# A first norm for two batches only, the other six and three pieces of preparation woven into the attention

## The chip, the cores and the metric

The kernel runs on one NeuronCore of a Trainium2 chip. The metric is device time in microseconds (us) of one execution, as a median over executions. A core has five instruction streams that run side by side and wait for one another by semaphores: TensorE (PE, matrix products and transposes through the array), VectorE (DVE), ScalarE (ACT, functions from tables, copies, scalings), GpSimd (POOL) and SyncE (SP, which issues most DMA transfers). PEld is PE's loading of weights, which overlaps its matmuls. Each stream is worked off in its own order.

## The reference, cut to what matters

Four layers act on x of 8 batches with 512 tokens of 128 values. Each layer does

```python
xn = _layernorm(x, axis=-1)      # (x - mean) / sqrt(var + 1e-5)
s = attention(xn)
g = _silu(ffn(xn))
x = x + s * g
```

The change concerns the first layer and preparation for later ones. The attention of layer 0 has 16 heads of 8 values and a sliding window of 64 tokens: a block of 64 queries sees its own and the previous block of keys, masked, with a softmax over 128 keys, and a projection out. The feed-forward part of layer 0 multiplies by six 128x128 weights, which come as integers and are decoded as `q / 7.5 - 1`, times a scale per group of 16, plus a low-rank product. The attention of layer 1 mixes each token with the one before by three vectors of weights. The attention of layer 3 needs per head a few scalars (softplus, sigmoid, reciprocals of six parameters).

## The kernel before, in words

x lies transposed in SBUF, 128 values on the partitions and 4096 tokens along the free axis, as do xn (normed) and s (attention out). Eight loads of 256 KB fill x. A tile of the norm is one batch, 512 tokens, so there are eight tiles.

**The first norm**, `layer_norm`: for each tile PE multiplies four blocks of 128 tokens by a centring matrix `cmat`, which gives rows of tokens less their mean in PSUM (`ps_c`); ACT squares them (`sq`), DVE sums (`var`) and adds epsilon, POOL takes the power -0.5 (`rstd`), DVE multiplies (`row`), PE transposes back (`ps_t`) and ACT copies into `xn`. The tiles follow one another with the later parts two and three tiles behind. PE, DVE, ACT and POOL run it in program order (`in_order`).

**Beside it**: `l0_decode` turns the integers of the six weights into `wt` by three DVE operations of 128x768. `l1.fill` has ACT issue the loads of the expert weights (`m1_w13`, `m1_w2`), then compute `td`, `rest`, the six mixing weights `wm` and a halved weight. `l3_scalars` stands in the source after the feed-forward part, but its operations are not held in order, and the scheduler puts them early: in the profile they run before the first scores (lines 2740 to 2777). The loads of weights for layers 2 and 1 (`L2Consts`, `L1Consts`) stand on SP's queue ahead of the layer-0 weights `a0_w`.

**The attention**, `l0_attention`: every engine works in program order, which is written out by hand. A batch has eight units u; a unit is 128 queries by 8 heads. In unit u, in this order: `turned(u)` transposes the eight exponentiated score blocks on PE (`tp`), four to a bank, and ACT copies them out (`pt`); in every second unit DVE divides the finished sums (`rec`, `o`); `scores(u + 3)` has PE multiply (`sc`), DVE scale and mask (`e`) and take the maximum (`mx`), POOL subtract it; `out_rows` transposes `o` (`tpo`, `ot`); ACT takes the exponential of unit u + 2; `weigh(u)` multiplies with the values on PE (`av`); in unit 1 of a batch `finish` projects the batch before (`ps_o`, `s`). Last, `next(todo)` does one step of the projections of the next batch: in unit 0 the keys (`ps_k`, then four pieces `kb` in turn by DVE and ACT, the first two here and the other two in unit 1), in unit 2 the queries (`ps_q`, `q`), in units 3 and 4 the values (`ps_v`, `vw`). The generator `l0_low_rank` adds the low-rank products to `wt` in unit 6 of the later batches. All of tp, tpo, ps_k, ps_q, ps_v and ps_o take their banks from one pool of three PSUM banks (`p_t`); scores have two buffers of two banks, the sums one bank.

Numbers of units below are of the whole attention (u = 0 to 63), "unit 0 to 7" within a batch is u modulo 8. Nearly all lines carry L83 in the profile, since the helper that keeps program order issues them; groups are told apart by the names of tiles.

Of the kernel before, what the change touches and what calls it, by code (L numbers as in the profile page):

```python
# [9 lines left out]
F32 = mybir.dt.float32  # L10
# [17 lines left out]
class Net:  # L28
# [110 lines left out]
        self.nc.gpsimd.tensor_tensor(r, var, self.neg_half.to_broadcast([P, n]), ALU.pow)  # L139
        return r  # L140

    def layer_norm(self, x, xn, gamma=None, beta=None, banks=(5, 3), free=False):

        nc, tc = self.nc, self.tc
        K = TB // P
        pe, dve, act, pool = (
            e if free else self.in_order(e)
            for e in (nc.tensor, nc.vector, nc.scalar, nc.gpsimd)
        )
        with tc.tile_pool(name="ln_s", bufs=3) as sp, tc.tile_pool(  # L150
            name="ln_p", bufs=banks[0], space=PSUM
        ) as pp, tc.tile_pool(name="ln_t", bufs=banks[1], space=PSUM) as tp:
# [38 lines left out]

            for t in range(NTB + 3):
                if t < NTB:
                    centre(t)
                    spread(t)
                if 2 <= t < NTB + 2:
                    scale(t - 2)
                if t >= 3:
                    turn(t - 3)
                    keep(t - 3)  # L200
# [46 lines left out]
            )  # L247


def l0_attention(net, xn, s_out, p0, w, bias):  # L250


    nc, tc = net.nc, net.tc
# [3 lines left out]
    with ExitStack() as st:  # L257
# [146 lines left out]
            scores(u)  # L404
        act.activation(e[0], e[0], AF.Exp)
        act.activation(e[1], e[1], AF.Exp)
        todo = iter(())
        for u in range(N + 2):
            if u < N and u % U == 0 and u // U + 1 < B:
# [14 lines left out]
            if u >= U and u % U == 1:  # L424
                finish(u // U - 1)
            next(todo, None)
            if u == 4 * U:
                low = net.prep.l0_low_rank(
                    p0, lambda name: p_t.tile([P, S], F32, tag="t", name=name), pe, dve, act
                )  # L430
            if u > 4 * U and u % U == 6:
                next(low, None)


L0_FFN = (
# [288 lines left out]
class L1Consts:  # L724
    E = 8

    def __init__(self, net, st):
        nc, tc, E = net.nc, net.tc, self.E
        self.net = net
        self.p1 = p1 = st.enter_context(tc.tile_pool(name="a1_c", bufs=1))  # L730
        self.rw = net.load(p1, "m1_r")
        self.eb = p1.tile([P, E], F32, tag="eb", name="eb")
        nc.sync.dma_start(self.eb, net.ins["m1_eb"].partition_broadcast(P))
# [3 lines left out]

    def fill(self):
        net, nc, p1, E = self.net, self.net.nc, self.p1, self.E
        act = net.in_order(nc.scalar)  # L740
        self.w13 = net.load(p1, "m1_w13", act)
        self.w2 = net.load(p1, "m1_w2", act)

        w, par = self.w, self.par
        self.td = td = p1.tile([P, 1], F32, tag="td", name="td")
        act.activation(td, par[:, 0:1], AF.Exp)
        act.activation(td, td, AF.Copy, scale=-1.0)
        self.tf = par[:, 1:2]
        self.wm = wm = p1.tile([P, 3, 2, P], F32, tag="wm", name="wm")
        self.rest = rest = p1.tile([P, 3], F32, tag="rest", name="rest")  # L750
        act.activation(rest, par[:, 2:5], AF.Identity, scale=-1.0, bias=net.ones[:, 0:1])
        for i in range(3):
            act.activation(wm[:, i, 0, :], w[:, i, :], AF.Copy, scale=par[:, 2 + i : 3 + i])
            act.activation(wm[:, i, 1, :], w[:, i, :], AF.Copy, scale=rest[:, i : i + 1])
        act.activation(w[:, 3, :], w[:, 3, :], AF.Copy, scale=0.5)

        def counting(tag, shape, pattern, base=0, channel=0):
            i = p1.tile(shape, I32, tag=tag + "_i", name=tag + "_i")
# [17 lines left out]
        self.keep = p1.tile([P, E, NTILE], F32, tag="keep", name="keep")  # L776
        nc.gpsimd.memset(self.keep, 1.0)
        nc.gpsimd.memset(self.keep[:, :, 0:1], 0.0)


def l1_layer(net, x, xn, s_out, consts, l2):
# [552 lines left out]
class L2Consts:  # L1334
# [4 lines left out]
    def __init__(self, net, st):  # L1339
# [2 lines left out]
            self.W, self.H, self.HD, self.LH, self.LD, self.NL, self.CH  # L1342
        )
        self.net = net
        self.p1 = p1 = st.enter_context(tc.tile_pool(name="a2_c", bufs=1))
        self.w = net.load(p1, "a2_w")
        self.wqt = net.load(p1, "a2_qt")
        self.wg = net.load(p1, "a2_g")
# [1312 lines left out]
class Prepared:  # L2661
# [26 lines left out]
            )  # L2688
        self.f0_wt = p1.tile([P, 6, P], F32, tag="wt", name="wt")

    def l0_decode(self):
        nc, wt, qw, sc = self.net.nc, self.f0_wt, self.qw, self.sc
        nc.vector.tensor_copy(wt, qw)
        nc.vector.tensor_scalar(wt, wt, 1.0 / 7.5, -1.0, ALU.mult, ALU.add)
        nc.vector.tensor_tensor(wt, wt, sc, ALU.mult)

    def l0_low_rank(self, p1, bank, pe, dve, act):

# [28 lines left out]
            dve.tensor_scalar(w0, w0, mean, None, ALU.subtract)  # L2727
            yield

    def l3_scalars(self):  # L2730

        net, nc, p1 = self.net, self.net.nc, self.p1
        H, DH = 16, 64
# [3 lines left out]
        )  # L2737
        sp = p1.tile([P, 4, H], F32, tag="sp", name="sp")
        raw = par[:, 1:5, :]
        nc.vector.scalar_tensor_tensor(sp, raw, -1.0, raw, ALU.mult, ALU.min)  # L2740
        nc.scalar.activation(sp, sp, AF.Exp)
        nc.scalar.activation(sp, sp, AF.Ln, bias=net.ones[:, 0:1])
        nc.vector.scalar_tensor_tensor(sp, raw, 0.0, sp, ALU.max, ALU.add)
        sig2, eta2, gam2, nu = (sp[:, i, :] for i in range(4))

        def vec(tag):
            return p1.tile([P, H], F32, tag=tag, name=tag)

        mu, nmu, v_e2, v_0, coef = vec("mu"), vec("nmu"), vec("v_e2"), vec("v_0"), vec("coef")
        nc.scalar.activation(mu, par[:, 0, :], AF.Exp, scale=-1.0)  # L2750
        nc.vector.tensor_scalar(mu, mu, 1.0, None, ALU.add)
        nc.vector.reciprocal(mu, mu)
        nc.vector.tensor_scalar(mu, mu, 1e-4, None, ALU.add)
        nc.vector.tensor_scalar(nmu, mu, -1.0, None, ALU.mult)

        nc.vector.tensor_scalar(v_e2, nmu, 2.0, None, ALU.mult)
        nc.vector.reciprocal(v_e2, v_e2)
        nc.vector.tensor_tensor(v_e2, v_e2, sig2, ALU.mult)
        nc.vector.tensor_tensor(v_0, eta2, gam2, ALU.add)
        nc.vector.tensor_tensor(v_0, v_0, v_e2, ALU.subtract)  # L2760
        nc.vector.tensor_scalar(coef, nu, float(DH), -0.5, ALU.add, ALU.mult)
        nc.vector.tensor_tensor(coef, coef, par[:, 5, :], ALU.mult)


        norm_0 = vec("norm_0")
        nc.vector.tensor_tensor(norm_0[0:64], nu[0:64], v_e2[0:64], ALU.mult)
        nc.vector.tensor_tensor(norm_0[64:128], nu[64:128], v_0[64:128], ALU.mult)
        cs, ncs, inv_cs, g_v = vec("cs"), vec("ncs"), vec("inv_cs"), vec("g_v")


        nc.vector.scalar_tensor_tensor(cs, coef, -1.0, coef, ALU.mult, ALU.max)
        nc.vector.tensor_scalar(cs, cs, 1e-18, 2e-18, ALU.is_lt, ALU.mult)
        nc.vector.tensor_tensor(cs, cs, coef, ALU.add)
        nc.vector.tensor_scalar(ncs, cs, -1.0, None, ALU.mult)
        nc.vector.reciprocal(inv_cs, cs)
        nc.vector.tensor_scalar(g_v, coef, -1.0, -0.5 * DH, ALU.mult, ALU.add)
        nc.vector.tensor_tensor(g_v, g_v, inv_cs, ALU.mult)
        self.scalars = nu, nmu, v_e2, v_0, norm_0, ncs, inv_cs, g_v


def network(tc, ins, out):
    with ExitStack() as ctx:
# [12 lines left out]
        with tc.tile_pool(name="prep_0", bufs=1) as p0:  # L2795
            w0, b0 = net.load(p0, "a0_w"), net.load(p0, "a0_b")
            prep.l0_load(p0)
            net.layer_norm(x, xn)
            prep.l0_decode()
            l2.fill()  # L2800
            l1.fill()
            l0_attention(net, xn, s, p0, w0, b0)
            l0_ffn(net, x, xn, s, l1)
        prep.l3_scalars()
        l1_layer(net, x, xn, s, l1, l2)
        st1.close()
        l2_layer(net, x, xn, l2)
# [82 lines left out]
```

## Time and profile before

| What | us |
|---|---|
| median of 12 runs (lowest, highest) | 2343.67 (2334.29, 2349.53) |
| the profiled execution, its own time | 2333.47 |
| its span | 2331.7 |
| busy PE / DVE / ACT / POOL in the span | 2172.8 / 1995.2 / 1857.1 / 1577.5 |
| first norm's first product | 4.08 |
| first scores of the attention | 42.00 |
| last projection out of the attention (s) | 315.40 |

Lines of the profile give start and length in us, the engine, the line of the kernel, the operation, the tiles written and read with shapes, and in brackets how long the engine sat idle before and what released it. "PEclk" is the clock that was granted to PE, as a share of full speed. A matmul in float32 shows as two PE instructions, a transpose as one. The profile is one execution; its own time differs from the median of the runs.

### The profile page before, as it was taken

To read this page: it belongs to the slowest core of one execution; us is meant where nothing else is said; L and a number is where in the kernel's file an instruction comes from. 1 tells how busy PE (TensorE), PEld (TensorE's weight loads), DVE (VectorE), ACT (ScalarE), POOL (GpSimd) and SP (SyncE) were. 2 spreads that over 40 slices of the span, in tenths; PEclk is the share of its full clock that TensorE was granted. 3 is DMA by queue.
4 is the path that set the end of the run, shared out by engine and by line. 5 is a ranking of instruction groups with operands and counts; after the bars stand their busy time and mean duration, and the time that the engine had idled before them with its cause. 6 is when DMAs were issued, how large, how long until landed. Compare 5 with 4: busy or idle time off the path is not lost.

```text
span 2331.7 us, 48954 instructions
## 1 busy us (share of the span) xinstructions
PE 2172.8 (93%) x17762; PEld 1518.3 (65%) x17762; DVE 1995.2 (86%) x3579; ACT 1857.1 (80%) x3906; POOL 1577.5 (68%) x1414
## 2 busy tenths in 40 slices
PE   5999998999987999769999999999999999999888
PEld 4666676556534666537777767777777777777676
DVE  4677778875787999679999999999999999999655
ACT  4666665555544899849999999999999999999875
POOL 4444435355276788666788887888887888887555
PEclk7999988999998999999999999999999999999999
DMA  4000001012210000144444344344443444433100
GB/s 144 2 2 2 2 1 37 9 54 71 44 49 13 7 17 16 57 115 107 109 107 109 94 105 110 101 106 107 105 105 102 99 111 112 104 95 87 40 1 37
DMA packets 91617, 156.94 MB, mean 67 GB/s; under 512 B 20144, under 2 KB 44464, under 8 KB 91120
## 3 DMA queue, kind: packets, MB, share of 16 engines
q1 hardware_dynamic: 86736, 140.95, 23.1%
q0 software_dynamic: 4352, 8.92, 1.6%
q10 hardware_dynamic: 288, 3.93, 0.4%
q8 instruction: 142, 2.33, 0.4%
q14 instruction: 99, 0.81, 0.1%
HBM read 30.52 MB, written 12.06 MB: 18 GB/s over the span
## 4 chain that ended last, share of the span: by engine, by line
PE 56%; DVE 31%; POOL 4%; issue 4%; ACT 3%; DMA 1%; SPq 1%; DVEq 0%; ACTq 0%; POOLq 0%
PE sc L83 11%; DVE sc L83 8%; DVE y L83 6%; DVE r L83 6%; PE ps_av L83 6%; PE ps_u L83 5%; PE tp L83 5%; PE ps_kq L83 5%; PE ps_ab L83 3%; PE av L83 3%; PE ps_n L83 3%; DVE mx L83 2%; DVE e L83 2%; PE ps_v L83 2%; PE ps_y L83 1%
## 5 line engine op out<-in xcount | busy, mean ns | idle before, releaser
L83 POOL TENSOR_TENSOR ek<-E,kn 128x512 f32<-128x512 f32 (+3 forms) x512 | 434.7, 871 | 204.3 <-DMA kn<-nr 191.1
L83 POOL TENSOR_TENSOR e<-e,mx 128x1024 f32<-128x1024 f32 x112 | 212.2, 1901 | 181.6 <-DVE mx L83 91.5
L83 PE MATMUL sc<-r 128*128 128x512 f32 (+3 forms) x1024 | 308.5, 445 | 25.0 <-DVE y L83 22.2
L83 POOL TENSOR_TENSOR r<-r,rs 128x1024 f32<-128x1024 f32 x128 | 304.2, 2377 | 19.9 <-DMA rs<-r 17.2
L83 PE MATMUL ps_av<-u,at 128*128 128x128 f32 x2560 | 308.2, 276 | 0.8 <-ACT o L83 0.8
L83 PEld LDWEIGHTS ps_av<-u,at 128*128 128x128 f32 x2560 | 297.5, 193 | 1.1 <-ACT o L83 1.1
L83 ACT ACTIVATE y<-y,mn 128x384 f32<-128x384 f32 (+3 forms) x512 | 288.6, 569 | 3.8 <-DVE mn L83 3.0
L83 PEld LDWEIGHTS sc<-r 128*128 128x128 f32 x1024 | 164.8, 191 | 188.8 <-issue 113.9
L83 DVE SCALAR_TENSOR_TENSOR y<-sc,qn,V 128x512 f32<-128x512 f32 (+3 forms) x512 | 246.5, 544 | 9.1 <-DVE sc L83 0.5
L83 DVE CUSTOM_DVE_ANT_0 y<-y,ps_g,ncs 128x384 f32<-128x384 f32 (+3 forms) x512 | 253.2, 540 | 0.0
L83 PEld LDWEIGHTS tp<-ident,y 128*128 128x128 f32 x1280 | 161.5, 141 | 115.5 <-issue 49.2
L83 ACT ACT_TABLE_LOAD x175 | 224.5, 1283 | 6.0 <-DVE ex L83 2.1
L83 PE MATMUL tp<-ident,y 128*128 128x128 f32 x1280 | 203.9, 274 | 3.4 <-ACT o L83 1.4
L83 ACT COPY at<-tp 128x512 f32<-128x512 f32 (+1 forms) x384 | 195.3, 509 | 6.1 <-PE tp L83 3.3
L83 DVE TENSOR_TENSOR sc<-sc,EF 128x1280 f32<-128x1280 f32 x128 | 191.9, 1499 | 4.4
L83 DVE SCALAR_TENSOR_TENSOR sc<-sc,ek 128x1280 f32<-128x1280 f32 x128 | 189.7, 1482 | 3.8 <-issue 2.4
L83 POOL TENSOR_TENSOR s<-s,o 128x512 f32<-128x512 f32 x120 | 154.1, 1284 | 32.5 <-ACT o L83 32.5
L83 ACT ACTIVATE y<-y 128x1280 f32<-128x1280 f32 x128 | 163.4, 1277 | 5.2 <-DVE y L83 4.5
L83 DVE TENSOR_TENSOR r<-sn,ps_kq 128x1024 f32<-128x1024 f32 x128 | 155.2, 1212 | 8.0 <-PE ps_vo L2038 4.4
L83 DVE TENSOR_TENSOR r<-ct,ps_kq 128x1024 f32<-128x1024 f32 x128 | 155.1, 1211 | 0.0
L83 ACT ACTIVATE sq<-ps_kq 128x1024 f32<-128x1024 f32 x128 | 131.6, 1028 | 29.2 <-PE ps_kq L83 29.1
L83 ACT ACTIVATE e<-e 128x1024 f32<-128x1024 f32 x112 | 117.3, 1062 | 41.0 <-POOL e L83 40.5
(465 smaller groups left out, 5002.2 us busy)
## 6 DMA issues: line engine op xcount, KB each, us to landing
rs<-r SPq DMA_DIRECT2D x256, 256.0 KB, 3.8
kn<-nr SPq DMA_DIRECT2D x512, 64.0 KB, 2.0
yrows<-yy SPq DMA_DIRECT2D x36, 128.0 KB, 1.8
ct<-trig SPq DMA_DIRECT2D x16, 256.0 KB
EF<-E SPq DMA_DIRECT2D x16, 256.0 KB, 2.9
EF<-E SPq DMA_DIRECT2D x16, 192.0 KB
m_w<-m_w ACTq DMA_DIRECT2D x1, 2560.0 KB, 10.2
x<-x SPq DMA_DIRECT2D x8, 256.0 KB, 5.5
```

The source lines that it names most:

```text
L83: ins = op(*args, **kwargs)
```

## The change

Only the first two batches go through `layer_norm`. The other six are normed inside the attention, in parts at the ends of units: for batch b the centring product (`centre`, with a copy of the rows to SBUF, `lc`) at the end of u = 8(b - 3) + 7 (u = 1 for b = 2), the square one unit later, the sum and root (`spread`) another unit later, the scaling by ACT in four pieces (`scale_rows`) two units after that, and the transposes and copy into xn (`turn_rows`) at the end of u = 8(b - 2) + 6. The banks come from the pool p_t. DVE's multiplication `row` is replaced for these batches by ACT's copies with a scale.

`l0_decode` (its last step now on POOL), the mixing weights (`mixing`) and `l3_scalars` become generators; from u = 8 on, units 2, 4 and 5 of a batch each do one step of them. The steps fall at u = 10, 12, 13 (decode), 18, 20, 21, 26, 28, 29 (mixing) and 34, 36, 37, 42, 44, 45, 50, 52 (scalars). The loads for layers 2 and 1 come after those for layer 0, and the expert weights are issued by SP and not by ACT.

```diff
-    def layer_norm(self, x, xn, gamma=None, beta=None, banks=(5, 3), free=False):
+    def layer_norm(self, x, xn, gamma=None, beta=None, banks=(5, 3), free=False, n=NTB):
...
-            for t in range(NTB + 3):
-                if t < NTB:
+            for t in range(n + 3):
+                if t < n:
                     centre(t)
                     spread(t)
-                if 2 <= t < NTB + 2:
+                if 2 <= t < n + 2:
                     scale(t - 2)
...
-def l0_attention(net, xn, s_out, p0, w, bias):
+def l0_attention(net, x, xn, s_out, p0, w, bias, l1):
...
+        mid, sqs, std = {}, {}, {}
+
+        def centre(b):
+            ps = p_t.tile([P, 4, P], F32, tag="t", name="ps_c")
+            for k in range(4):
+                pe.matmul(
+                    ps[:, k, :], lhsT=x[:, ts(4 * b + k, P)], rhs=net.cmat,
+                    start=True, stop=True,
+                )
+            mid[b] = p2.tile([P, 4, P], F32, tag="lc", name="lc")
+            act.copy(mid[b], ps)
+
+        def square(b):
+            sqs[b] = p2.tile([P, 4, P], F32, tag="sq", name="sq")
+            act.activation(sqs[b], mid[b], AF.Square, scale=net.inv_root)
+
+        def spread(b):
+            var = p2.tile([P, 4], F32, tag="var", name="var")
+            std[b] = p2.tile([P, 4], F32, tag="rstd", name="rstd")
+            dve.tensor_reduce(var, sqs.pop(b), AX.X, ALU.add)
+            dve.tensor_scalar(var, var, EPS, None, ALU.add)
+            pool.tensor_tensor(std[b], var, net.neg_half.to_broadcast([P, 4]), ALU.pow)
+
+        def scale_rows(b):
+            for k in range(4):
+                act.activation(
+                    mid[b][:, k, :], mid[b][:, k, :], AF.Copy, scale=std[b][:, k : k + 1]
+                )
+
+        def turn_rows(b):
+            ps = p_t.tile([P, 4, P], F32, tag="t", name="ps_t")
+            for k in range(4):
+                pe.transpose(ps[:, k, :], mid[b][:, k, :], net.ident)
+            act.copy(xn[:, ts(b, S)], ps.rearrange("p k q -> p (k q)"))
+
+        norms = {}
+        for b in range(2, B):
+            c = U * (b - 3) + 7 if b > 2 else 1
+            for part, at in (
+                (centre, c), (square, c + 1), (spread, c + 2), (scale_rows, c + 4),
+                (turn_rows, U * (b - 2) + 6),
+            ):
+                norms.setdefault(at, []).append((part, b))
+
+        def early():
+            yield from net.prep.l0_decode(dve, pool)
+            yield from l1.mixing(act)
+            yield from net.prep.l3_scalars(dve, act)
+
+        rest = early()
...
             next(todo, None)
+            for part, b in norms.get(u, ()):
+                part(b)
+            if u >= U and u % U in (2, 4, 5):
+                next(rest, None)
...
     def fill(self):                          # of L1Consts
-        act = net.in_order(nc.scalar)
-        self.w13 = net.load(p1, "m1_w13", act)
-        self.w2 = net.load(p1, "m1_w2", act)
...
+        self.w13 = net.load(p1, "m1_w13")
+        self.w2 = net.load(p1, "m1_w2")
...
+    def l0_decode(self, dve, pool):
+        wt, qw, sc = self.f0_wt, self.qw, self.sc
+        dve.tensor_copy(wt, qw)
+        yield
+        dve.tensor_scalar(wt, wt, 1.0 / 7.5, -1.0, ALU.mult, ALU.add)
+        yield
+        pool.tensor_tensor(wt, wt, sc, ALU.mult)
+        yield
...
+    def l3_scalars(self, dve, act):
...
+        dve.scalar_tensor_tensor(sp, raw, -1.0, raw, ALU.mult, ALU.min)
+        act.activation(sp, sp, AF.Exp)
+        act.activation(mu, par[:, 0, :], AF.Exp, scale=-1.0)
+        yield
+        act.activation(sp, sp, AF.Ln, bias=net.ones[:, 0:1])
+        yield
...
             prep.l0_load(p0)
-            net.layer_norm(x, xn)
-            prep.l0_decode()
+            l2.load()
+            l1.load()
+            net.layer_norm(x, xn, n=2)
             l2.fill()
             l1.fill()
-            l0_attention(net, xn, s, p0, w0, b0)
+            l0_attention(net, x, xn, s, p0, w0, b0, l1)
             l0_ffn(net, x, xn, s, l1)
-        prep.l3_scalars()
```

More of the change, by code (lines that the diff above doesn't have):

```diff
@@ L432, in l0_attention @@
                 next(low, None)
+        for _ in rest:
+            pass
 L0_FFN = (
@@ L729, in __init__, with load @@
         self.net = net
-        self.p1 = p1 = st.enter_context(tc.tile_pool(name="a1_c", bufs=1))
+        self.p1 = st.enter_context(tc.tile_pool(name="a1_c", bufs=1))
+    def load(self):
+        net, nc, p1, E = self.net, self.net.nc, self.p1, self.E
         self.rw = net.load(p1, "m1_r")
@@ L739, in fill @@
         net, nc, p1, E = self.net, self.net.nc, self.p1, self.E
-        act = net.in_order(nc.scalar)
-        self.w13 = net.load(p1, "m1_w13", act)
-        self.w2 = net.load(p1, "m1_w2", act)
[L744 to L755, printed above, removed]
+        self.w13 = net.load(p1, "m1_w13")
+        self.w2 = net.load(p1, "m1_w2")
         def counting(tag, shape, pattern, base=0, channel=0):
@@ L778, in fill, with mixing @@
         nc.gpsimd.memset(self.keep[:, :, 0:1], 0.0)
+    def mixing(self, act):
+        net, p1, w, par = self.net, self.p1, self.w, self.par
+        self.td = td = p1.tile([P, 1], F32, tag="td", name="td")
+        act.activation(td, par[:, 0:1], AF.Exp)
+        act.activation(td, td, AF.Copy, scale=-1.0)
+        yield
+        self.tf = par[:, 1:2]
+        self.wm = wm = p1.tile([P, 3, 2, P], F32, tag="wm", name="wm")
+        self.rest = rest = p1.tile([P, 3], F32, tag="rest", name="rest")
+        act.activation(rest, par[:, 2:5], AF.Identity, scale=-1.0, bias=net.ones[:, 0:1])
+        yield
+        for i in range(3):
+            act.activation(wm[:, i, 0, :], w[:, i, :], AF.Copy, scale=par[:, 2 + i : 3 + i])
+            act.activation(wm[:, i, 1, :], w[:, i, :], AF.Copy, scale=rest[:, i : i + 1])
+            yield
+        act.activation(w[:, 3, :], w[:, 3, :], AF.Copy, scale=0.5)
+        yield
 def l1_layer(net, x, xn, s_out, consts, l2):
@@ L1344, in __init__, with load @@
         self.net = net
-        self.p1 = p1 = st.enter_context(tc.tile_pool(name="a2_c", bufs=1))
+        self.p1 = st.enter_context(tc.tile_pool(name="a2_c", bufs=1))
+    def load(self):
+        net, p1 = self.net, self.p1
         self.w = net.load(p1, "a2_w")
@@ L2689, in l0_load @@
         self.f0_wt = p1.tile([P, 6, P], F32, tag="wt", name="wt")
[L2691 to L2695, printed above, removed]
+    def l0_decode(self, dve, pool):
[3 more added lines that the diff above has]
+        dve.tensor_scalar(wt, wt, 1.0 / 7.5, -1.0, ALU.mult, ALU.add)
+        yield
+        pool.tensor_tensor(wt, wt, sc, ALU.mult)
+        yield
     def l0_low_rank(self, p1, bank, pe, dve, act):
@@ L2728, in l0_low_rank @@
             yield
-    def l3_scalars(self):
+    def l3_scalars(self, dve, act):
         net, nc, p1 = self.net, self.net.nc, self.p1
@@ L2739, in l3_scalars @@
         raw = par[:, 1:5, :]
[L2740 to L2744, printed above, removed]
         def vec(tag):
@@ L2749, in l3_scalars @@
         mu, nmu, v_e2, v_0, coef = vec("mu"), vec("nmu"), vec("v_e2"), vec("v_0"), vec("coef")
[L2750 to L2762, printed above, removed]
+        yield
+        dve.scalar_tensor_tensor(sp, raw, -1.0, raw, ALU.mult, ALU.min)
+        act.activation(sp, sp, AF.Exp)
+        act.activation(mu, par[:, 0, :], AF.Exp, scale=-1.0)
+        yield
+        act.activation(sp, sp, AF.Ln, bias=net.ones[:, 0:1])
@@ new lines, in l3_scalars @@
+        yield
+        dve.scalar_tensor_tensor(sp, raw, 0.0, sp, ALU.max, ALU.add)
+        sig2, eta2, gam2, nu = (sp[:, i, :] for i in range(4))
+        yield
+        dve.tensor_scalar(mu, mu, 1.0, None, ALU.add)
+        dve.reciprocal(mu, mu)
+        dve.tensor_scalar(mu, mu, 1e-4, None, ALU.add)
+        dve.tensor_scalar(nmu, mu, -1.0, None, ALU.mult)
+        dve.tensor_scalar(v_e2, nmu, 2.0, None, ALU.mult)
+        dve.reciprocal(v_e2, v_e2)
+        dve.tensor_tensor(v_e2, v_e2, sig2, ALU.mult)
@@ L2765, in l3_scalars @@
+        yield
+        dve.tensor_tensor(v_0, eta2, gam2, ALU.add)
+        dve.tensor_tensor(v_0, v_0, v_e2, ALU.subtract)
+        dve.tensor_scalar(coef, nu, float(DH), -0.5, ALU.add, ALU.mult)
+        dve.tensor_tensor(coef, coef, par[:, 5, :], ALU.mult)
+        yield
         norm_0 = vec("norm_0")
-        nc.vector.tensor_tensor(norm_0[0:64], nu[0:64], v_e2[0:64], ALU.mult)
-        nc.vector.tensor_tensor(norm_0[64:128], nu[64:128], v_0[64:128], ALU.mult)
+        dve.tensor_tensor(norm_0[0:64], nu[0:64], v_e2[0:64], ALU.mult)
@@ L2768, in l3_scalars @@
+        dve.tensor_tensor(norm_0[64:128], nu[64:128], v_0[64:128], ALU.mult)
         cs, ncs, inv_cs, g_v = vec("cs"), vec("ncs"), vec("inv_cs"), vec("g_v")
[L2771 to L2776, printed above, removed]
@@ L2777, in l3_scalars @@
-        nc.vector.tensor_tensor(g_v, g_v, inv_cs, ALU.mult)
+        yield
+        dve.scalar_tensor_tensor(cs, coef, -1.0, coef, ALU.mult, ALU.max)
+        dve.tensor_scalar(cs, cs, 1e-18, 2e-18, ALU.is_lt, ALU.mult)
+        dve.tensor_tensor(cs, cs, coef, ALU.add)
+        dve.tensor_scalar(ncs, cs, -1.0, None, ALU.mult)
+        dve.reciprocal(inv_cs, cs)
+        dve.tensor_scalar(g_v, coef, -1.0, -0.5 * DH, ALU.mult, ALU.add)
+        dve.tensor_tensor(g_v, g_v, inv_cs, ALU.mult)
         self.scalars = nu, nmu, v_e2, v_0, norm_0, ncs, inv_cs, g_v
+        yield
```

## The prediction

> **What bounds the kernel now.** I read the page first (span 2331.7 us; PE busy 93%), then busy time by stage, because the change touches only the first 312 us: the first norm, the attention of layer 0 and what is prepared beside them. After it the order of instructions on PE, DVE and ACT is the same in both kernels. The last fence lists the stages: a full batch of attention (eight units), the last batches, and two stretches of 4 us. Columns: stretch, length, then busy us (and instructions) of PE, PEld, DVE, ACT, POOL, then the granted clock of PE.
>
> The timeline of the start comes next (start, length, engine, line, operation, idle before and its releaser):
> ```profile
> 10.90 4.00 POOL L83 TENSOR_TENSOR rstd<-var,neg_half 128x4 f32<-128x4 f32 x4
> 12.74 0.66 PE L83 MATMUL ps_t<-ident,row 128*128 128x128 f32 x4 [3.10 <-DVE row L83]
> 13.43 0.59 ACT L83 COPY xn<-ps_t 128x512 f32<-128x512 f32 x1 [3.16 <-PE ps_t L83]
> ...
> 30.36 1.13 PE L83 MATMUL ps_k<-xn,a_w 128*128 128x512 f32 x2 [0.68 <-ACT xn L83]
> ...
> 35.76 0.76 ACT L83 ACTIVATE kb<-ps_k,kbias,hm 128x512 f32<-128x512 f32 x1
> 36.53 1.28 ACT L2742 ACT_TABLE_LOAD   x1
> 38.20 1.28 ACT L2750 ACT_TABLE_LOAD   x1
> 39.61 0.76 ACT L83 ACTIVATE kb<-ps_k,kbias,hm 128x512 f32<-128x512 f32 x1
> 40.42 1.65 PE L83 MATMUL ps_v<-a_w,xn 128*128 128x128 f32 x6 [7.19 <-ACT kb L83]
> 42.00 2.01 PE L83 MATMUL sc<-kb,q 32*64 32x512 f32 x16
> ```
> The first projection (ps_k) waits until eight tiles are normed, 30.36; then ACT has mixing weights and the scalars' two table loads in front of kb, so PE idles 7.19 us and the first scores start at 42.00.
>
> In the attention PE is the bound, with waits in two units of each batch:
> ```profile
> 120.51 0.30 PE L83 MATMUL tpo<-ident,o 128*128 128x128 f32 x1 [0.24 <-DVE o L83]
> 123.78 0.78 ACT L83 ACTIVATE kb<-ps_k,kbias,hm 128x512 f32<-128x512 f32 x1 [0.76 <-DVE kb L83]
> 124.46 1.06 ACT L83 COPY pt<-tp 128x512 f32<-128x512 f32 x2
> 125.09 1.13 PE L83 MATMUL av<-vw,pt 128*64 128x9 f32 x32 [0.30 <-ACT pt L83]
> 127.39 0.74 DVE L83 TENSOR_SCALAR s<-ps_o,a_b 128x512 f32<-128x512 f32 x1
> 128.19 0.66 PE L83 MATMUL tp<-ident,e 128*128 128x128 f32 x4 [0.48 <-DVE s L83]
> 128.77 0.25 DVE L83 RECIPROCAL rec<-av 128x16 f32<-128x16 f32 x1
> ```
> There av waits for pt, which stands behind kb on ACT; then the transposes wait for s, and the next out-transposes for rec, behind s and kb on DVE. PE is idle only 1.35 of 31.85 us.
> ```profile
> 98.34:130.19 31.85, 30.50 (x408) 19.97 (x408) 23.55 (x28) 20.80 (x34) 15.18 (x8) 1.00 0.01 2
> 257.60:290.00 32.40, 31.59 (x412) 21.05 (x411) 23.47 (x30) 20.48 (x33) 14.25 (x8) 0.95 0.01 2
> 256.00:260.00 4.00, 3.45 (x44) 1.90 (x43) 3.38 (x6) 2.08 (x5) 1.90 (x1) 1.00 0.00 0
> 260.00:264.00 4.00, 4.00 (x26) 2.60 (x28) 1.40 (x2) 2.15 (x3) 1.90 (x1) 0.57 0.01 4
> ```
> After these waits the clock fell to 0.57 once, at 260.
>
> **The start: what is removed.** POOL's constants keep its first root at 10.90 whatever the change does. Two roots of 1.0 us end at 12.9; row takes 0.69, the second transposes 13.7 to 14.4, the second xn copy ends at 15.05. The weights a0_w now stand ninth on SP's queue, behind eight x loads that issue from 0.79 to 4.50; the load that stood there before was there by 10.9, so it is in time. So ps_k starts at 15.1. Its bias follows 1.16 later (30.36 to 31.52), then four kb pieces in turn, DVE and ACT, 0.8 each: the fourth starts at 18.7. Before, the scores began 2.39 after the fourth (39.61 to 42.00): 21.1, say 21.2. Saved: **20.8 us**. Of it 15.3 is the earlier ps_k, 5.5 the wm, td, sp and mu work taken out of ACT's way. The unknown is the clock: PE now idles from about 7.9 to 12.7, and an idle of 4.9 (15.7 to 20.6) was followed by 0.50. Then the transposes cost 0.9 more and ps_k 1.0 (2.08 where 55.35 shows it at 0.50): 18.6 saved. The other end: 21.5, with 0 to 1.0 more if the first scores, 1.06 each at full clock, do not run at 0.50 as they did. I take 20.8 and 0.5 of that 1.0. The w13 and w2 loads move from ACT's queue to the end of SP's; nothing on SP waits behind them until xrows, some 300 us later. The f0 scales and layer-2 loads move past each other on SP, with first readers in the attention or later.
>
> **The attention: what is added, per batch** (on the batch of 98.34, unit by unit).
> - Unit 6: four transposes ps_t, 0.47 of PE (tp of four, half of 1.0). ACT's xn copy, 0.53, delays pt to 116.8, still in time for av. **+0.47.**
> - Unit 7: ps_c, eight PE instructions like the ps_v of eight, 1.0. ACT's lc copy fits. The 0.3 that tpo waited for o goes. **+0.7.**
> - Unit 0: Square, 0.53 of ACT, stands between kb and pt, exactly where av waits. With the shifts so far PE's wait at av grows from 0.35 to 1.15. **+0.8.**
> - Unit 1: DVE gets the reduce and the addition, 0.69 + 0.08, between kb and rec. PE was idle here anyway; some shows at tpo. POOL's root, 1.0, lies before a subtraction that waits for mx. **+0.2.**
> - Unit 3: four scalings on ACT. The nearest row is wm, 128x128, one every 0.29 (34.10 to 34.39): 1.2, ahead of pt. ACT idles 0.8 and 0.59 there, so av is late by **0.28**.
>
> Sum 2.45. Five batches (3 to 7) have all of it: 12.3. Batch 2 falls into the start, where tpo waited 1.20 at 64.39 for kb: ps_c lies in that wait, lc and Square cost 0.6 and 0.3, and the last ps_t 0.3 more: 1.5 (0.5 to 3, the upper end with ps_c at half clock). The last batch has none.
>
> **The single steps.** Ln's load, Ln and the load back now stand in unit 37 on ACT: 1.28 + 0.35 ahead of pt (av +0.4), 1.28 ahead of e, then xn and rows ahead of the next pt (+0.6): 1.0. Four small DVE operations (0.5) in unit 45 stand before rec: 0.5. The other steps (cast 0.56 and scale 0.55 on DVE; the multiplication, 0.95 on DVE before, on POOL between 1.28 for 512 columns and 1.90 for 1024; wm at 0.6 a pair) fall where their engine idles 1 to 2 us a unit: 0.3. If that cover were gone they would cost 6 (decode 1.1 on DVE, 2.6 on ACT, some 20 small DVE operations at 0.12). Together **1.8** (1 to 5).
>
> The Trainium skill's page "ScalarE: Activation LUTs", section "What ACT_TABLE_LOAD costs", adds a drain of 1.38 us to each load of 1.28; the row shows kb ending at 36.52 and the load starting at 36.53, so none is visible. By the page two loads would cost 2.8 more.
>
> **The clock.** This is what decides. The drop at 260 cost 0.95 on ps_q (2.07 against 1.13) and 0.78 on tp (1.82 against 1.04): 1.7. It came after waits of 0.48 and 0.15 that every batch has, once in six; the single wait of 1.20 at 64.39 was followed by one too. With the change the waits in units 1 and 2 grow to 1.15, 0.5 and 0.5. Drops in none to all of five batches: 0 to 8.5. I take two more: **3.4**.
>
> The page "TensorE: Matmul & The Clock Gate", section "HAM oscillation — how this bites in real kernels", asks only that PE have no gap above some 3.4 us; by that none would come, and the sum would be 3.4 lower. The row at 260 speaks against it.
>
> **Sum.** -20.8 - 0.5 + 12.3 + 1.5 + 1.8 + 3.4 = **-2.3 us**. The profiled execution took 2333.47 (span 2331.7 and 1.8 around it), 10.2 below the median of 12 runs, 2343.67; the sum made against it gives 2331.2, and carried to the median 2341.4, 0.1% faster. A measurement of this kernel can tell about 0.2%, 4.7 us, from no change.
>
> **Rivals.**
> - *No drops: faster.* All as worked out but no further clock drop: -5.7, 2338.0. If Square, reduce and scaling also vanish in waits, the attention pays 9.0 of PE less the 1.5 that tpo waited, and 1.0 for tables: -12.8, 2330.9. For it: ACT is busy 20.80 and DVE 23.55 of 31.85. Against: Square stands ahead of the one pt that is already late. I take 2335.
> - *Clock drops in every batch: slower.* From waits above about 0.6 us in one stretch (the sum at 257 to 260) PE runs a stretch at half clock in units 2 and 3: five times 1.7 is +2.8 in the sum; if low activity holds the clock down for a second stretch, as from 42 to 58, five times 3.4 gives +11.3. I take 2351. For it: 260 and 64.39; against: three to four batches with the same waits kept 1.00.
> - *The steps find no cover: slower.* The 6 us all on the path, not 0.3: +3.4 in the sum, and with one more drop +5.1: 2348.8.
> - That the change doesn't do what it says is unlikely: all streams in the attention stand in program order, and the built order has each part at its unit. L2742's loads are indeed ahead of the first scores before.
>
> **How the numbers follow.** Forecast 0.37; no drops 0.34; drops in every batch 0.23; no cover 0.06. Within 0.2% is the forecast's own 2337 to 2348 nearly whole; the first rival is mostly beyond 0.2%, the others as a rule. Faster 0.35, same 0.37, slower 0.28. The range runs from the far end of the first rival, 2331, to the second's, 2355; the forecast's own is 2337 to 2348.
>
> **What would show it.** First sc at 21.2 (18.6 saved if ps_t shows 1.1 us, at 0.50). A batch period of 34.3 against 31.85, longer where the clock falls behind units 1 and 2. av in unit 1 waiting about 1.15 for pt, with sq right before pt on ACT. Two table loads between unit 37 and 38. The end of attention (last s, 315.4 before) at about 313. I am wrong if the period stays below 33 with a steady clock (first rival), if 0.5 shows in every batch (second), or if sc starts after 24.

## The result and the profile after

The changed kernel took 2371.43 us (median of 15 runs, 2349.05 to 2377.63) where the kernel before took 2341.26 beside it (62 runs): ratio 1.0115, 95% interval 1.0099 to 1.0131 (it is the ratio of the mean times; that of the two medians would be 1.0129). It is 1.2% slower; the forecast was 0.1% faster, and its range ended at 2355. The profiled execution took 2367.65, its span is 2365.9 against 2331.7, with PE's mean clock at 0.955 against 0.972.

The start came as worked out. The timeline of the changed kernel (columns as before the change):

```profile
12.74 2.11 PE L83 MATMUL ps_t<-ident,row 128*128 128x128 f32 x8 [4.79 <-DVE row L83]
15.52 2.07 PE L83 MATMUL ps_k<-xn,a_w 128*128 128x512 f32 x2 [0.68 <-ACT xn L83]
20.20 0.78 ACT L83 ACTIVATE kb<-ps_k,kbias,hm 128x512 f32<-128x512 f32 x1 [0.88 <-DVE kb L83]
22.10 1.11 PE L83 MATMUL sc<-kb,q 32*64 32x512 f32 x16
```

The first scores start at 22.10 instead of 42.00: 19.9 us won. From there to the end of the last s it takes 321.5 us instead of 274.1. All of the win and 27.5 us more are lost inside the attention. (The rest of the span is 6.7 us longer, in the same order of instructions; in four profiles further down that rest differs by 6.5 with no pattern, so nothing is read into it.) Busy time by stage, a batch per line (columns: stretch, length, then busy of PE, PEld, DVE, ACT, POOL, then the granted clock; a batch took 31.85 before, the last line 55.82):

```profile
47.57:86.69 39.12, 35.76 (x422) 24.14 (x420) 25.74 (x32) 23.80 (x41) 17.20 (x10) 0.89 0.01 2
...
123.25:157.38 34.13, 31.87 (x423) 21.33 (x420) 24.38 (x30) 24.33 (x46) 16.18 (x9) 1.00 0.01 2
157.38:195.04 37.66, 36.22 (x424) 23.66 (x421) 24.91 (x30) 25.14 (x46) 16.18 (x9) 0.87 0.01 2
...
232.90:278.77 45.87, 41.09 (x420) 26.61 (x416) 29.53 (x43) 22.39 (x39) 15.18 (x8) 0.78 0.00 1
278.77:343.60 64.83, 60.49 (x644) 42.27 (x641) 35.42 (x54) 29.95 (x48) 20.87 (x11) 0.73 0.01 2
```

The batch whose clock stayed at 1.00 took 34.13, and the prediction's period was 34.3. Every other batch is longer and has a lower clock; the two longest are the two in which the scalars' DVE steps run. Over all eight stretches PE is busy 294.2 us (257.8 before) and idle 27.3 (16.3 before). Of the 47.4 us more, 11.0 are waits, 8.8 are work (six batches by 1.47), and the remaining 27.6 are put down to more of the same work at half clock.

What comes before the drops is seen in unit 1 of a batch:

```profile
114.80 0.62 ACT L83 ACTIVATE sq<-lc 128x512 f32<-128x512 f32 x1
115.94 1.13 PE L83 MATMUL av<-vw,pt 128*64 128x9 f32 x32 [1.02 <-ACT pt L83]
117.00 2.04 PE L83 MATMUL ps_o<-ot,a_w 128*128 128x512 f32 x2
```

Square stands ahead of pt, av waits 1.02, and the next product, ps_o, lasts 2.04 where it lasts 1.13 at full clock. Five batches have this wait, and behind each of the five, within 2 us or after some 6 us with two more waits of 0.4, the clock is at half, four times for 3.4 us and once for 10.2. Not every wait has this: one of 0.78 (at 215.57) and one of 0.83 (at 275.71) are followed by full clock. And in the scalars' steps, of DVE, POOL and PE:

```profile
244.42 1.90 POOL L83 TENSOR_TENSOR e<-e,mx 128x1024 f32<-128x1024 f32 x1 [2.18 <-PE tp L83]
244.65 1.70 DVE L83 TENSOR_SCALAR mu<-mu 128x16 f32<-128x16 f32 x1
...
249.88 1.90 POOL L83 TENSOR_TENSOR e<-e,mx 128x1024 f32<-128x1024 f32 x1 [3.57 <-DVE v L83]
249.92 1.89 DVE L83 TENSOR_SCALAR coef<-sp 128x16 f32<-128x16 f32 x1
...
252.66 0.30 PE L83 MATMUL tpo<-ident,o 128*128 128x128 f32 x1 [3.71 <-DVE o L83]
```

An operation on 16 values a partition, 0.17 us a few lines further on, lasts 1.70 and 1.89: it starts while POOL subtracts and ends when POOL does (244.42 + 1.90 = 246.32; 249.88 + 1.90 = 251.78). o stands behind both (the first holds up the next e and with it mx, the second the division), and PE waits 3.71. What follows, by stretches of 4 us:

```profile
252.00:256.00 4.00, 3.34 (x41) 2.89 (x41) 2.83 (x5) 1.90 (x3) 0.86 (x1) 0.70 0.02 4
256.00:260.00 4.00, 4.00 (x18) 1.99 (x17) 1.15 (x4) 2.13 (x3) 1.03 (x1) 0.50 0.00 0
...
264.00:268.00 4.00, 4.00 (x41) 2.14 (x42) 1.91 (x2) 1.90 (x3) 0.97 (x1) 0.50 0.02 4
```

PE is busy all the time and at half clock. The trace of before had shown the collision too, in a row that the prediction passed over:

```profile
278.97 1.90 POOL L83 TENSOR_TENSOR e<-e,mx 128x1024 f32<-128x1024 f32 x1 [1.18 <-PE tp L83]
279.17 0.29 DVE L83 TENSOR_REDUCE mean<-wt 128x1 f32<-128x128 f32 x1
279.67 1.27 DVE L83 TENSOR_SCALAR wt<-wt,mean 128x128 f32<-128x128 f32 x1
```

The TENSOR_SCALAR ends with the subtraction (280.94 and 280.87); the TENSOR_REDUCE of the same 128x128 beside the same subtraction took 0.29.

### The profile page after: what moved, and what is told of

Read it like the earlier page. It is cut to its first block, busy times and chain, and to the rows that moved or that the text cites. A ratio compares the mean times of both kernels' runs of the same rounds, so it can differ in the third digit from the quotient of the medians.

```text
span 2365.9 us, 48955 instructions
## 1 busy us (share of the span) xinstructions
PE 2209.9 (93%) x17762; PEld 1541.8 (65%) x17762; DVE 1995.5 (84%) x3572; ACT 1865.0 (79%) x3936; POOL 1580.6 (67%) x1415
## 4 chain that ended last, share of the span: by engine, by line
PE 58%; DVE 27%; POOL 5%; ACT 4%; issue 4%; DMA 1%; SPq 1%; POOLq 0%; ACTq 0%; DVEq 0%
PE sc L83 11%; DVE sc L83 8%; DVE y L83 6%; DVE r L83 6%; PE ps_av L83 6%; PE tp L83 5%; PE ps_u L83 4%; PE ps_kq L83 4%; PE av L83 3%; PE ps_ab L83 3%; PE ps_n L83 2%; PE ps_v L83 2%; PE ps_y L83 1%; DVE mx L83 1%; PE ps_p L83 1%
## 5 line engine op out<-in xcount | busy, mean ns | idle before, releaser
L83 DVE SCALAR_TENSOR_TENSOR e<-sc,maskFalse 128x1024 f32<-128x1024 f32 (+1 forms) x96 | 90.4, 952 | 77.6 <-PE sc L83 77.5
```

The source lines that it names most:

```text
L83: ins = op(*args, **kwargs)
```

## The experiments

Two theories at first: **A (port)**, DVE operations that meet POOL's subtraction; **B (weave)**, the norm's steps that let PE wait about 1 us behind units 0 and 1, with the clock's drops. The kernel before took from 2344 to 2368 us in the different sets of runs, so ratios are compared, each to the kernel before run beside it. Each measured kernel had 4 to 12 runs. "Change" below is the changed kernel.

**1. The norm woven, the single steps as before.** Edit of the change: `early()` and its calls gone, the old prologue for decoding, mixing weights and scalars.

> Theory A (port): the change lost its gain to the single steps, because small DVE operations of the scalars that are issued while POOL subtracts last until the subtraction ends (1.70 to 1.89 us instead of 0.1 to 0.2), o comes late, PE waits up to 3.7 us and then runs some 20 us at half clock. In the changed kernel the last full batch and the tail were 13.1 and 9.0 us above the worked periods. Rival B (weave): the six norms make PE wait about 1 us for pt in each batch, and the clock drops behind it; that alone is the loss. This kernel weaves the six norms but makes the single steps as the kernel before did, in the prologue. By A the time is some 20 us below the changed kernel, about 2350 (the first scores start some 3 to 5 us later than 22.1, since ACT has the mixing weights first), and the batches show 34 to 38 with no long tail. By B it stays within 8 us of the changed kernel, 2363 to 2375.

Measured: 1.0121 (1.0079 to 1.0164), 2391.88 us. As a ratio that lies where B had it, but it says nothing for B, since the first scores start at 44.28 and not 3 to 5 us behind 22.10, because ACT stands in front of kb for parameters whose load is now late on SP:

```profile
36.83 0.20 ACT L83 ACTIVATE td<-a_p 128x1 f32<-128x1 f32 x1 [16.83 <-DMA a_p<-a_p]
```

So moving the mixing weights off the head of ACT's queue is what lets the new load order pay. The attention answers the question all the same: its five batches are 39.11, 36.55, 34.14, 37.62 and 38.09 (change: 39.12, 36.56, 34.13, 37.66, 37.86), and then 35.13 and 60.40 where the change has 45.87 and 64.83. The norm makes the first five, the scalars the excess of the last two.

**2. The single steps woven, the norm as before.** `net.layer_norm(x, xn)` for all tiles, no `norms`.

> All eight tiles are normed up front as in the kernel before; only the single steps are woven in. First scores at about 36.5 (42.0 less the 5.5 that the steps took out of ACT's way). By A (port) the last two batches are still some 20 us long, so the time is 14 to 18 us above the kernel before: about 2356, 1.006. By B (weave) it is 4 to 6 us below it: about 2336, 0.998. If both are needed (the steps only hurt where the norm has used up the slack) it lies near the kernel before, 2341 to 2346.

Measured: 1.0002 (0.9973 to 1.0031), neither A's 1.006 nor B's 0.998. First scores at 29.84, 6.7 us earlier than expected, and the attention takes 300.2 us instead of 274.1: a win at the start and a larger loss at the end, without the norm, give the small difference that "both are needed" had foretold. Batches with decoding and mixing are 31.85 to 31.88, as before: those steps cost nothing. The one with the scalars' table loads is 33.04 (before: 32.56): the loads cost 0.5. The next is 48.48: PE waits 3.97 for o, then 34 us at clock 0.50 follow.

**3 and 4. The scalars behind the attention; and all single steps between e and mx.**

```diff
-            yield from net.prep.l3_scalars(dve, act)      # 3: run after the loop over units
+            # 4: in scores(u + 3), unit as before
+            dve.scalar_tensor_tensor(e[u], ...)
+            next(step, None)
+            dve.tensor_reduce(mx, e[u], ...)
```

> The changed kernel, with the scalars' steps run behind the attention's loop instead of at ends of units 37 and later; the decoding, mixing weights and six norms stay woven. By A (port) the stalls of 3.7 and 1.35 us for o and the half-clock stretches at 252 to 270 and 292 to 318 vanish: the attention ends near 322 instead of 342.9, and the time is 15 to 20 us below the changed kernel, 2351 to 2356. By B (weave) the batches stay at 37 to 38 and it is at most 5 us below it. A third, C (tables): the Exp and Ln table loads on ACT are the loss; then this kernel gains as by A, which the next one tells apart.

> The changed kernel, with each single step emitted in the same units, but on DVE between e and mx of the unit's scores, where POOL has not started its subtraction; ACT's steps and table loads stay in the attention. By A (port) the small operations take 0.1 to 0.2 us, and the time is 12 to 20 us below the changed kernel, 2351 to 2359. By C (tables on ACT) and by B (weave) it is within 5 us of the changed kernel, 2366 to 2375, and the last batches keep their excess of 13 and 9 us.

Measured: 1.0031 (1.0010 to 1.0053) and 1.0015 (0.9992 to 1.0037), both as A has it. In the fourth the operation of 1.70 us lasts 0.17, with table loads and order as in the change, and the subtraction starts behind it: it is the meeting with POOL, not the tables.

```profile
245.63 0.17 DVE L83 TENSOR_SCALAR mu<-mu 128x16 f32<-128x16 f32 x1
248.02 1.90 POOL L83 TENSOR_TENSOR e<-e,mx 128x1024 f32<-128x1024 f32 x1 [3.47 <-ACT pt L83]
```

In the third the steps behind the loop give back some: the first c of the feed-forward part starts 5.9 us after s ends, 1.0 in the fourth. Both still have the norm's drops, and one collision is left: the norm's own `var` addition in the first woven batch lasts 1.47, o is 1.34 late and 17 us at half clock follow (from 57.6; in the third 24 us).

**5. Square earlier and the spread between e and mx, on top of 4.**

> The changed kernel with three of its steps moved inside their units: single steps between e and mx on DVE, as in the kernel before this one; the reduce and the addition of the spread between e and mx too (in the first woven batch the addition lasted 1.47 us beside POOL's subtraction, o came 1.33 us late and the clock stayed at half for 4 to 22 us); and Square ahead of unit 0's projection step, where ACT waits for the first kb, instead of between kb and pt. Theory A+B (both losses come from short waits, and each brings a stretch of half clock): av in unit 1 waits 0.3 to 0.4 instead of 1.02, most drops behind units 1 and 2 vanish, periods near 34.3, attention ends near 308 to 312; ratio to the kernel before 0.994 to 0.998. If the clock drops come from the added work itself and not from these waits, the periods stay at 36 to 38 and the ratio at 1.000 to 1.003.

Measured: 1.0015 (0.9983 to 1.0047), a miss, and no different from the fourth. Square ahead of kb delays kb, and with it s: the waits became 0.50 to 0.93 for pt and up to 0.87 for s, and drops came as before. A wait was moved, not removed.

**6. The prices by themselves, in the kernel before.** One ACT Square in unit 0 (a); three small DVE operations behind mx in unit 5 (b), and three of another kind (c); batches 1 to 7:

```diff
+                act.activation(junk, xn[:, 0:S], AF.Square)              # a
+                dve.tensor_scalar(little, mx16, 2.0, None, ALU.mult)     # b, three times
+                dve.tensor_reduce(little[:, 0:1], mx16, AX.X, ALU.max)   # c, three times
```

> The kernel before, with one more thing: an ACT Square of 128x512 into an unused tile behind unit 0's projection step, in batches 1 to 7, the place where the change puts its own. Nothing is added to PE. It measures the price of the wait for pt alone. If the wait costs only itself, av in unit 1 waits 0.9 to 1.0 instead of 0.30, so seven times 0.6 to 0.7: 4 to 5 us, 1.002. If each such wait also brings the clock to half for 4 to 6 us (theory B), 3 us more for each: 20 to 28 us, 1.009 to 1.012.

> The kernel before, with three small DVE operations (TENSOR_SCALAR from SBUF to SBUF, 128x16, 0.17 us by themselves) at the end of unit 5 of batches 1 to 7, behind mx, where POOL's subtraction begins. By theory A one of the three lasts until the subtraction ends, 1.5 to 1.9 us; o comes late, tpo waits 1.3 to 2 us instead of 0.25, and behind it the clock stays at half for 10 us or more: 7 times 1.3 to 2 and 3 to 10 for the clock, 30 to 80 us, 1.013 to 1.034. If the small operations only cost their own time (the long ones being an accident of the scalars' chain), 7 times 0.3: 2 us, 1.001.

> As the kernel with the three small TENSOR_SCALAR operations, but the three are TENSOR_REDUCE 128x16 to 128x1, at the same place. If what holds them is a port that only some of DVE's operations share with POOL (in the traces TENSOR_REDUCE mx and var keep their length beside a subtraction), they take 0.1 to 0.2 us each and the time is within 5 us of the kernel before, 1.000 to 1.002. If any small DVE operation behind mx is held up, it is as long as with TENSOR_SCALAR, 1.013 to 1.034.

Measured: Square 0.999 (0.9952 to 1.0028), TENSOR_SCALAR 1.0282 (1.0245 to 1.0319), TENSOR_REDUCE 1.0098 (1.0056 to 1.0139). The timeline of (b), then that of (c):

```profile
112.70 2.18 DVE L83 TENSOR_SCALAR little<-mx 128x16 f32<-128x16 f32 x3
112.95 1.90 POOL L83 TENSOR_TENSOR e<-e,mx 128x1024 f32<-128x1024 f32 x1 [2.16 <-ACT pt L83]
115.51 0.30 PE L83 MATMUL tpo<-ident,o 128*128 128x128 f32 x1 [2.34 <-DVE o L83]
```

```profile
121.53 0.57 DVE L83 TENSOR_REDUCE little<-mx 128x1 f32<-128x16 f32 x3
122.73 0.30 PE L83 MATMUL tpo<-ident,o 128*128 128x128 f32 x1 [0.73 <-DVE o L83]
```

Three TENSOR_SCALAR take 2.18 together and end with POOL's 1.90; three TENSOR_REDUCE in the same place take 0.57. That it depends on the kind of operation is shown, as a shared port would have it. Twenty-one operations of 0.17 us cost 67 us by the ratio. The reduces missed their expected time on the other account: a wait for o of 0.73 instead of 0.25 was followed, in two of six such waits, by some 20 us of half clock. (Another 20 us at half clock, from 66.0, follow a wait of 1.19 that the kernel before has too, there with 3.4 us; these are not the reduces' doing.) For Square, av waited 0.82, and the clock fell behind four of six such waits; the attention is 8 us longer in the profile, but the runs allow at most 0.3% (7 us). So the waits for pt alone cost less than the 20 to 28 us of theory B.

**7. The norm's steps moved to free units; and the wait filled.** The first moves centre to unit 5, Square to 7, the spread between e and mx of unit 4, scalings to 5, and the single steps between e and mx of units 2, 4 and 6. The second is kernel 4 with more buffers for pt, so that the last ones are still there, and with

```diff
+            if U <= u < N and u % U == 1:
+                weigh(u - 1, last)        # the av products of unit 0 again, same values
             if u < N:
                 weigh(u, pts)
```

> The changed kernel with the norm's steps moved to units where the engines have room: the row sums on PE at the end of unit 5, Square at unit 7, reduce and addition between e and mx of unit 4 (an even unit, where o has gone before), the four scalings at unit 5, the transposes at unit 6 as before; the single steps between e and mx of units 2, 4 and 6. So no new work stands ahead of pt in units 0 and 1, nor behind mx. Theory A+B: the only waits left are those of the kernel before (0.30 for pt, 0.48 for s, 0.25 for o), and drops come as seldom as there; PE has 1.47 more a batch: periods 33.3 to 34, attention ends at 302 to 310, ratio 0.993 to 0.997. If the drops come from the added work as such, periods stay at 36 or more and the ratio above 1.000.

> The kernel with the single steps between e and mx (everything else as changed, so Square stands ahead of pt in unit 0 and av of unit 1 finds pt 1.02 us late), and one thing more: in unit 1 of batches 1 to 7 PE repeats the av products of unit 0, the same values into the same place, 1.1 us ahead of its own av. It adds 7.9 us of PE work and leaves the late pt as it is; it fills the wait. If it is the idle PE that brings the clock down, the drops behind unit 1 vanish (five or six of them, 2 to 4 us each): periods near 34.5 and a ratio of 0.994 to 0.999, below that of the same kernel without it (1.0015). If the clock falls for another reason, the periods stay at 36 to 38 and the ratio at 1.001 to 1.004.

Measured: 1.0050 (1.0030 to 1.0070) and 1.0059 (1.0029 to 1.0088), misses in time. The respread kernel has two batches of 33.30 at clock 1.00 (31.85 + 1.45), so the norm's work costs what was worked out; but the logarithm's tables now met the transposes' copy in unit 38 (tp waited 2.10 for xn), and the low-rank steps, still behind mx, met the subtraction (1.27 us; o 0.94 and 1.67 late). In the filled kernel the batches behind the first are:

```profile
98.80:132.94 34.14, 32.90 (x456) 22.35 (x452) 24.88 (x32) 23.39 (x43) 17.98 (x10) 1.00 0.01 2
132.94:167.08 34.14, 32.90 (x456) 22.35 (x452) 24.23 (x30) 24.53 (x46) 16.19 (x9) 1.00 0.01 2
```

With 1.1 us more work a batch, and pt as late as before, no drop follows unit 1 any more, though the two waits of 0.4 in unit 2 are still there (kernel 4 had one behind each of its five waits of 1.02, with 36.43 and 35.09 for two of these batches). Its time went elsewhere: 34 us of half clock behind `var`'s collision, 24 behind a late o, and the kernel as a whole is slower than kernel 4; that the idle time brings the clock down is shown by the trace in this place only.

**8. What is left taken away, and filled.** On top of the respread kernel: the scalars' exponentials in unit 60, their logarithm behind the last pt and DVE's chain behind the last o, the low-rank steps between e and mx of units 34, 38, 42 and 46. Then the same with fillers: twelve unneeded products in front of the first transposes, and half of `weigh(u - 1)` again in unit 1 and the last two units (again with more buffers for pt).

> The respread kernel without the three waits that it still had: the scalars' exponentials between e and mx of unit 60, their logarithm behind the last pt, their DVE chain behind the last o (no scores and no subtraction run there any more), and the low-rank steps between e and mx of units 34, 38, 42 and 46, so that their TENSOR_SCALAR no longer meets a subtraction. Both causes at work (port and idle): the waits of 2.10, 0.94 and 1.67 and the half-clock stretches behind them, 24 us in all at 210 to 224, 256 to 260 and 294 to 302, go; the attention ends 12 to 18 us earlier than the respread kernel's 328, near 312; ratio 0.996 to 1.000. If drops come just as often after the short waits that the kernel before has too, the ratio stays at 1.002 to 1.005.

> The last kernel, with work that is not needed put on PE where it would wait: twelve row-sum products (into a bank that nobody reads) in front of the first transposes, where PE waits 3.2 us for the first exponential; and half of the previous unit's av products again (0.55 us, the same values into the same place) ahead of av in unit 1 of each batch, and in the last two units, where pt is 0.3 to 0.8 us late. PE has 6 us more to do, about 3 of it beyond its waits. If an idle PE brings the clock down, the half-clock stretches at 28 to 50 and at the end of the attention shorten, 5 to 12 us: ratio 0.991 to 0.997, below that of the kernel without the fillers. If not, it is 2 to 4 us slower than that one.

Measured: 0.9942 (0.9927 to 0.9958) and 0.9924 (0.9904 to 0.9944): faster than the kernel before by 0.6 and 0.8%, and than the change by more. The attention ends at 306.94 and 304.83. The fillers' own share does not stand out of the intervals.

**9. Two by two, on one chip.** The change again; the scalars moved alone; the norm moved alone; both (the decoding, mixing and low-rank steps stay as changed). The two edits, abridged:

```diff
-            yield from net.prep.l3_scalars(dve, act)
+            if u in (N - 4, N - 1):       # exponentials; logarithm; the DVE chain at u == N
+                next(scalars)
```
```diff
-                (centre, c), (square, c + 1), (spread, c + 2), (scale_rows, c + 4),
+                (centre, c + 5), (square, c + 7), (spread, t + 4), (scale_rows, t + 5),
+                # c = U * (b - 3), t = U * (b - 2); spread between e and mx
```

> The changed kernel itself, beside the next three on one chip. Ratio 1.010 to 1.013 as measured before; the attention ends 25 to 32 us later than in the kernel before.

> The changed kernel with one difference: the scalars' exponentials at the end of unit 60, their logarithm behind the last pt, their DVE chain behind the last o, where no subtraction runs. The norm stays as changed. If the scalars' share is what the runs up to now say (12 to 18 us), the ratio is 1.003 to 1.006, 14 us below the changed kernel; if the norm's waits are the whole loss, it is within 4 us of it.

> The changed kernel with the other difference alone: the norm's steps moved off units 7, 0 and 1 (row sums to unit 5, Square to 7, reduce and addition between e and mx of unit 4, scalings to 5). The single steps stay at ends of units, the scalars too. If the norm's waits with their clock drops cost what I now think (1.0 and 2 to 4 us of clock a batch), it is 8 to 16 us below the changed kernel, 1.004 to 1.008; the long half-clock stretches behind the scalars, at the last two batches, stay.

> Both differences together; the decoding, the mixing weights and the low-rank steps stay where the change has them. If the two shares add up, 22 to 32 us below the changed kernel, ratio 0.996 to 1.001. If removing either removes the other (the clock needs both), the ratio is that of the better of the two, 1.003 or more.

| | norm as changed | norm moved |
|---|---|---|
| scalars as changed | 1.0098 (1.0066 to 1.0129) | 1.0030 (1.0002 to 1.0057) |
| scalars at the end | 1.0031 (1.0007 to 1.0056) | 0.9966 (0.9939 to 0.9993) |

The scalars' place cost 0.67% (16 us), the norm's place 0.68% (16 us), both 1.32% (31 us): they add up, within intervals of some 0.3% each. The profiles, one execution each, split it otherwise: the attention took 321.5 us in the change, 317.0 with the scalars moved, 303.4 with the norm moved and 296.2 with both. With the scalars moved, 31 us at half clock came in that execution behind a wait of only 0.24; the shares of 16 us rest on the runs. The last two stretches of the kernel with both:

```profile
227.59:262.55 34.96, 33.16 (x419) 21.65 (x417) 25.30 (x33) 22.25 (x39) 16.19 (x9) 0.96 0.01 1
262.55:318.11 55.56, 52.13 (x647) 37.49 (x644) 36.83 (x67) 31.99 (x52) 20.87 (x11) 0.86 0.01 2
```

They were 45.87 and 64.83, and the instructions on PE are the same.

**10. The fillers in the kernel before.**

> The kernel before with the fillers of the last but one study alone: twelve products into a bank nobody reads in front of the first transposes, and half of the previous unit's av products again ahead of av in unit 1 of batches 1 to 7 and in the last two units. PE has 6 us more to do and waits some 3 us less. If idle PE is what brings the clock down, the half-clock stretches at 42 to 58 and 300 to 316 shorten and the ratio is 0.995 to 0.999; if the clock falls for another reason, 1.001 to 1.002.

Measured: 0.9986 (0.9956 to 1.0016), undecided. In the profile the six batches from 64.33 on all have clock 1.00, and the last stretch 0.96 (51.97 us) where it had 0.84 (55.82); the runs don't confirm a gain.

## Why the prediction was wrong

- *Start, 20.8:* right, 19.9, between it and the 18.6 given for ps_t at half clock. ps_t and ps_k did run at half clock (2.11 and 2.07), the first scores at full (1.11), the two things that the step had weighed.
- *Per batch 2.45, av's wait 1.15:* right where nothing else disturbs: 34.13 - 31.85 = 2.28, and 1.02. Its PE part, 1.47, is 1.45 in the respread kernel.
- *Batch 2, 1.5:* right for its first stretch (25.47 against 24.00), in part by luck, since the clock there was 0.76 against 0.64; but `var`'s addition met POOL's subtraction in the next (o 1.33 late), which the step did not have.
- **The single steps, 1.8 (1 to 5): the step that failed.** It counted each DVE operation at its own 0.12 to 0.17 us and looked for DVE's idle time. Decoding, mixing and tables were as cheap as it said. But the scalars' operations came just behind mx, where POOL begins, and one of each group lasted as long as the subtraction. The place cost 16 us, and even "cover gone" (6) was too small, since it priced the operations and not the collision. The Trainium skill's page "SBUF — State Buffer", section "Who interferes with whom", states the mechanism: DVE and GpSimd share a pair of ports as an exclusive lock, tensor_scalar in its two-port mode and tensor_tensor with two SBUF inputs contend for it, tensor_reduce never does on this chip. The rows agree on which operations are held: 2.18 against 0.57 for three, 1.77 for a TENSOR_TENSOR of 128x16 beside a subtraction. The ports themselves, and the mode that a TENSOR_SCALAR ran in, no run shows.
- **The clock, 3.4 (0 to 8.5): the second term that failed, in its size.** The mechanism (short waits, then half clock) was right, and it decided, as the text said. It allowed one drop of 1.7 us a batch at units 1 and 2. (The waits that it named before the drop at 260 come to 0.55 in its own row, 3.45 busy of 4.00, and not to 0.63.) The attention lost 27.6 us more to half clock than before: half of 3.4 us (four times) and 10.2 us (once) behind the wait in unit 1 of five batches, and half of 17 and 24 us behind the two late o of the scalars. Moving the norm alone won 16 us, while its work stayed. That move also takes away the meeting of `var` with the subtraction; how the 16 us divide between this and av's wait is open, and Square by itself cost the kernel before less than 7.
- *The rivals:* "drops in every batch" (2351) came nearest, and "no cover" (2348.8) named the other part; each was taken without the other and at too low a price, so the range ended 16 us short of the result.

## What to carry to other kernels

When work is put "into an engine's idle time", look at what the neighbouring engine does in that very moment: a TENSOR_SCALAR, or a TENSOR_TENSOR with both inputs in SBUF, that is issued just behind what releases a long POOL operation lasted until that one ended (a TENSOR_REDUCE did not), while the same operation a microsecond earlier, between e and mx here, costs its own time. Where PE is the bound, price each new wait of PE at several times its length, because the clock can fall behind it, and put new steps where they stand ahead of nothing that PE waits for. The same change with its steps in other places was 0.3 to 0.6% faster than before instead of 1.2% slower.

## What the runs showed of the hardware that was not expected

The length of half clock behind a wait is not set by the wait: after the same late o (1.32 to 1.34 us) of the first woven batch it lasted 3.4 us in the change, 17 and 24 in kernels 4 and 3, and 34 in the filled one; and 20 us in kernel 1, 14 in kernel 3 and 31 in the one with the scalars moved alone followed a wait of only 0.24 or 0.25, such as the kernel before has in each full batch at full clock. Read in windows of 0.2 us, the clock keeps to a grid: from 55 us to the end of the attention every stretch of half clock, in the traces of all these kernels, lasts a whole number of steps of some 3.41 us, from one to seventeen, and in the change they begin and end at 86.4, 89.8, 117.0, 120.4, 158.0, 161.4, 188.8, 199.0 and so on to 318.4, which is 68 steps behind the first. So the least price of a drop is half a step, 1.7 us, the price that the prediction had put on one. Yet two profiles of the change on different occasions agree within 0.02 us at the start of every batch, drops included. What sets the number of steps, and which wait is followed by a drop at all, stays open. The Trainium skill's page "TensorE: Matmul & The Clock Gate", section "HAM oscillation — how this bites in real kernels", gives the rule that PE have no idle gap above some 3.4 us; here waits of 1.02 were followed by drops in five of five batches (and in all five of kernels 1, 3, 4 and the one with the scalars moved alone), and filling just those waits with unneeded products removed the drops behind them.
